# Where ScalarE saves a scan's last column, when the FFN runs, and who multiplies behind a gelu

## The chip, the cores and the metric

The kernel runs on one core of a Trainium2 chip. The metric is the device time of one execution in microseconds (us), as the median of several runs. The core has five queues that work side by side and meet only at semaphores: TensorE (PE), VectorE (DVE), ScalarE (ACT), GpSimd (POOL), and SyncE (SP), which here issues nearly all DMAs. Each queue runs its own instructions strictly in program order.

## The reference

Eight images of 64 channels and 128x128 pixels go through two layers. The first is a filter whose nine taps per pixel come from a small convolution and a softmax. The second is a bidirectional Mamba block between convolutions, followed by a gated feed-forward part (FFN). What matters here is the scan of the Mamba block and the FFN:

```python
def selective_scan(u, dt, A, Bm, Cm, D, z):
    dt = jax.nn.softplus(dt)
    dA = jnp.exp(jnp.einsum('bdl,dn->bldn', dt, A))
    dBu = jnp.einsum('bdl,bnl,bdl->bldn', dt, Bm, u)
    ...
    _, hs = jax.lax.associative_scan(comb, (dA, dBu), axis=1)
    y = jnp.einsum('bldn,bnl->bdl', hs, Cm) + D[None, :, None] * u
    return y * jax.nn.silu(z)
...
xn = ln4d(x, norm2_w, norm2_b)
g = conv2d(xn, ffn_in_w, pad=0)
g = conv2d(g, ffn_dw_w, groups=2 * HID, pad=1)
g1, g2 = jnp.split(g, 2, axis=1)
g = jax.nn.gelu(g1, approximate=False) * g2
return x + conv2d(g, ffn_out_w, pad=0)
```

There are 128 inner channels `d` and 16 states `n` for each of 16384 pixels, two directions and two layers per image: for every channel and state a recurrence `h = dA * h + dBu` runs along the pixels, and its values are multiplied by `C` and summed over the states.

## The kernel before

**Chunks and steps.** The scans are the backbone. A chunk is 1024 pixels (`T`) of one image, layer and direction; there are 16 chunks per scan, 64 per image, 512 in all. A chunk's 128 channels times 16 states are 2048 rows, done as 16 steps of 128 rows (`U` = 16), so an image has 1024 steps (`IMAGE`). Step `u` of a chunk does the following:

- `decay` (L1226), two steps ahead: ScalarE writes `w = exp(dt * A)` into one of two PSUM tiles, in turn;
- `drive` (L1218): GpSimd computes `bu` for two steps in one instruction, some steps ahead, into four buffers;
- `scan` (L1245 forward, L1247 backward): VectorE runs the recurrence over `w` and `bu`, starting from the state column that the chunk before it left;
- `product`: the scan's values times `C`. Where `on_pool(u)` is true, the scan has written to SBUF (`hs`) and GpSimd multiplies one step later (L1264, L1266). Elsewhere the scan has written over `w` in PSUM, which GpSimd is not given, and VectorE multiplies (L1262);
- `keep` (L1269): ScalarE copies the last column of the scan, one value per row, to the state for the next chunk, 16 steps on;
- `collect` (L1284): PE sums two steps' products over the states.

`on_pool` (L1207) is true for steps 0, 2 and 6 of every eight, except right behind a step in which a gelu is planned (`gelu_times`): there VectorE keeps step 6's product. So a chunk has six products on GpSimd and ten on VectorE, in some chunks one more on VectorE.

**The order.** Nothing is left to a scheduler. `at(time, phase, fn)` puts every piece of work at a step and a phase, and at the end they are emitted in the order of step and phase: FEED, SCAN, MID, PROD, EXP, DECAY, REST. Within a step and phase the order is that of planning: the chunks first, in their order, then the rest. The position in this list decides the order in each engine's queue; waits between engines are put in by the tile layer where two instructions use the same tile. For a step whose product is on VectorE, product and copy both stand in phase PROD, product first; then come the decay for two steps on (EXP), outputs of other work on ScalarE (DECAY) and everything else (REST).

**Around the scan.** Each chunk is prepared during the 32 steps ahead of it: convolution, silu (L1119, and L1121 for the gate in the second of the two directions; planned at step 11 of a 16, REST) and softplus (L1148, step 2 of a 16, REST). Silu, softplus and gelu each need another ScalarE table than exp, so each loads a table before and the exp table again after (L68). Loads of `dup`, `dtp`, `bp` and `cp` for the next chunk go out on SP's queue at fixed steps.

**Beside the scan** run, on the same queues, the work of other images: `Front` (the first layer and norms of the next image, from step 593 - 24 of an image on, one piece every 24 steps), `Mix` (from 990 on, every 13 steps) and `Ffn` (`FFN_AT` = 1202, that is step 178 of the next image, every 24 steps, 16 pieces). Of the last image nothing is left to run beside, so its `Ffn` runs `alone`, after the scans, with other steps.

**One Ffn piece**, planned from step `a`: four window DMAs at a-4 and a-3 (`load`); the convolution of the first channel group at a to a+3, copied out at a+5 (`first_out`, L962); of the rest at a+6 to a+9; gelu at a+11 (`gelus`, L969 and L971, with the table loads); the rest's product at a+13 (`rest_times`, L976); the second group's convolution at a+14 to a+17; its two products at a+19 and a+21 (`times`, L979); two loads at a+16 (`load_x2`); the projection at a+21 (`project`, L994 to L1000), copied out and stored at a+23 (`add`, `store`).

Of the kernel before, what the change touches and what calls it, by code (L numbers as in the profile page):

```python
# [21 lines left out]
NCH = HALF // ROWS  # L22
# [14 lines left out]
FEED, SCAN, MID, PROD, EXP, DECAY, REST = range(7)  # L37

IMAGE = 4 * NT * U
FRONT_STEP, MIX_STEP, FFN_STEP = 24, 13, 24  # L40
FRONT_AT, MIX_AT, FFN_AT = 593, 990, 1202

SILU, SOFTPLUS, GELU = 11, 18, 11

# [11 lines left out]
def kernel(ctx: ExitStack, tc: tile.TileContext, a: dict, out: bass.AP):  # L56
# [6 lines left out]
    nc = tc.nc  # L63
    x = a["x"]
    B = x.shape[0]
# [122 lines left out]
    with tc.tile_pool(name="wspill", bufs=1) as fp, tc.tile_pool(name="wprep", bufs=2) as pp, \  # L188
            tc.tile_pool(name="wps", bufs=4, space=PSUM) as pps:
        with tc.manual_schedule():  # L190
# [161 lines left out]
            for l in range(DEPTH):  # L352
# [9 lines left out]
                for d in range(2):  # L362
                    cw, xdt, xbc, dtn, al, dp = dirs[2 * l + d]
                    taps = by_taps(inx2, cw, DI, KC)
                    for j in range(KC):
                        t = turned(taps[:, j, :], ident, P, DI)
                        at = j if d == 0 else KC - 1 - j
# [39 lines left out]
    def at(time, phase, fn, *args):  # L407
        steps.setdefault((time, phase), []).append((fn, args))
# [466 lines left out]
    class Ffn:  # L875
# [139 lines left out]
        def plan(self, a):  # L1015
            early = 12 if self.alone else 0
            at(a - 4 - early, REST, self.load, 0)
            at(a - 3 - early, REST, self.load, 1)

            if self.alone:  # L1020
                at(a - 6, REST, self.before_taps)
                at(a - 5, DECAY, self.before_taps_out)
                at(a - 5, REST, self.taps, 0)
                at(a - 2, REST, self.taps, 1)
                groups = ((0, 0, self.first_out, 2), (3, 1, self.times, 6))
                gelus, out = 3, 9
            else:
                groups = ((0, 0, self.first_out, 5), (6, 2, None, 0), (14, 1, self.times, 19))
                gelus, out = GELU, 21
            for t, g, end, to in groups:  # L1030
                for i in range(4):
                    at(a + t + (0 if self.alone else i), REST, self.conv, g, i)
                for h in range(2 if end else 0):
                    late = 0 if self.alone or end == self.first_out else 2 * h
                    at(a + to + late, MID if end == self.times else DECAY, end, h)
            at(a + gelus, REST, self.gelus)
            at(a + gelus + 2, MID, self.rest_times)
            at(a + out - 5, REST, self.load_x2)
            at(a + out, REST, self.project)
            at(a + out + 2, DECAY, self.add)  # L1040
            at(a + out + 2, REST, self.store)
# [7 lines left out]
            Ffn(b, c).plan(a + step * c)  # L1049


    gelu_times = {IMAGE * b + FFN_AT + FFN_STEP * c + GELU for b in range(B - 1) for c in range(NCH)}
    up, down = list(range(NT)), list(reversed(range(NT)))
    order = []
    for b in range(B):
# [4 lines left out]
    class Chunk:  # L1060
# [143 lines left out]
        def on_pool(self, u):  # L1204


            if u % 2 or u % 8 == 4 or self.t0 + u - 1 in gelu_times:  # L1207
                return False
            return True

# [55 lines left out]
                nc.gpsimd.tensor_tensor(out[:, ::-1], hs[:, ::-1], c[:, ::-1], ALU.mult)  # L1266

        def keep(self, u):
            nc.scalar.copy(self.column(u), self.last(self.hs.pop(u)))  # L1269

        def collect(self, k):

# [72 lines left out]
        def plan(self):  # L1345
            b = self.t0 - 2 * U

            def feed(t, fn, *args):
                if self.beside_front:
                    at(t, FEED, fn, *args)  # L1350
                else:
                    at(t - 1, REST, fn, *args)

            at(b + (5 if self.i == NCH - 2 else 3), REST, self.load_hn)
            for h in range(2):
                feed(b + 7 + h, self.conv, h)
                at(b + 7 + h, DECAY, self.conv_out, h)
                if self.second:
                    feed(b + 9 + h, self.gate, h)
                    at(b + 9 + h, DECAY, self.gate_out, h)  # L1360
                feed(b + 14 + h, self.step, h)
                at(b + 14 + h, DECAY, self.step_out, h)
            at(b + SILU, REST, self.silu)
            at(b + SOFTPLUS, REST, self.softplus)
            if self.second:
                at(b + 13, REST, self.store_gate)
            b = self.t0
            feed(b - 16, self.bc)
            at(b - 16, DECAY, self.bc_out)
            at(b - 14, REST, self.store_bc)  # L1370
            at(b - 13, REST, self.store_dt)
            at(b - 11, FEED, self.dtx)
            at(b - 10, REST, self.store_du)
            j0 = self.pairs[0][0] // 2
            at(b - 10, REST, self.load_states, "bp", j0)
            at(b - 8, REST, self.load_channels, "dup", 0)
            at(b - 6, REST, self.load_channels, "dtp", 0)
            at(b - 5, REST, self.load_states, "bp", 1 - j0)
            at(b - 4, REST, self.load_states, "cp", j0)
            at(b - 3, REST, self.load_channels, "dup", 1)  # L1380
            at(b - 2, REST, self.load_channels, "dtp", 1)
            at(b - 1, REST, self.load_states, "cp", 1 - j0)
            for k in range(U // 2):
                at(b + 2 * k - 5, REST, self.drive, k)
                at(b + 2 * k + 3 + (k % 4 == 0), REST, self.collect, k)
            for u in range(U):
                at(b + u - 2, EXP, self.decay, u)
                at(b + u, SCAN, self.scan, u)
                at(b + u + self.on_pool(u), FEED if self.on_pool(u) else PROD, self.product, u)
            for u in range(U):  # L1390
                at(b + u + self.on_pool(u), EXP if self.on_pool(u) else PROD, self.keep, u)
            for h in range(2):
                if self.second:
                    at(b + 8 * h + 1, REST, self.load_yf, h)
                    at(b + 8 * h + 6, REST, self.add_yf)
                    at(b + 8 * h + 7, REST, self.load_gate, h)
                if self.second:
                    at(b + 8 * h + 11, MID, self.y_out, h)
                else:
                    at(b + 8 * h + 10, DECAY, self.y_out, h)  # L1400
                    at(b + 8 * h + 11, REST, self.store_y, h)
            if not self.second:
                return
            b += U
            n = self.norm
            at(b + 2, REST, self.load_h)
            feed(b + 5, self.project)
            at(b + 6, DECAY, self.residual)
            at(b + 6, DECAY, self.square)
            if self.l == 0:  # L1410
                at(b + 7, REST, self.store_h)
            feed(b + 12, lambda: n.means(mm_tile, self.sq))
            at(b + 13, DECAY, n.means_out)
            feed(b + 17, n.spread, mm_tile)
            at(b + 19, MID, self.normed)
            if self.l:
                at(b + 20, DECAY, self.weighted)
            at(b + 20, REST, self.store_hn)
# [10 lines left out]
    for b in range(B):  # L1429
        a, last = IMAGE * b, b == B - 1  # L1430
# [36 lines left out]
```

## Time and profile before

| | us |
|---|---|
| median of 3 runs | 28348.76 (28341.41 to 28352.17) |
| the profiled execution | 28355.4 |
| its span, first to last instruction | 28353.5 |
| first scan starts | 386.1 |
| last scan starts | 27928.9 |
| one image's 1024 steps, images 2 to 7 | 3450.9 to 3457.7 |
| mean of one scan, L1245 and L1247 | 2.34 |
| VectorE's product, L1262 | 1.222 |
| GpSimd's product, L1264 and L1266 | 2.37 |
| GpSimd's drive, L1218 | 4.548 |
| ScalarE's decay, L1226 | 1.119 |
| ScalarE's copy of the last column, from `w` and from `hs` | 0.158 and 0.178 |
| a table load | 1.283 |

The rows of the profile give start, duration, engine, line, operation, and output and input tiles; in brackets stands how long the engine was idle before, and what ended that. `state<-w` is the copy behind a scan whose product VectorE makes, `state<-hs` one whose product GpSimd makes. The granted TensorE clock was 0.883 on average.

### The profile page before, as it was taken

The numbers are of one execution on the slowest core, as the hardware profiler recorded it, in microseconds if no ns is written. First come the engines' busy times: TensorE is split into PE (matmuls) and PEld (weight loads), VectorE is DVE, ScalarE is ACT, GpSimd is POOL, SyncE is SP. The second block draws the span as 40 slices with busy tenths as digits, with TensorE's granted clock in tenths as the row PEclk, the third lists the DMA queues.
The fourth block names the chain that finished last, engine by engine and source line by source line (L and its number), as shares of the span: only waits on it lengthen the run. The fifth ranks groups of instructions, "written<-read, shape, count | busy, mean of one in ns | idle before, by whom it ended". The sixth has DMA issues, their size and how long they took to land. (4 is left out here: it accounts for less than half of the span.)

```text
span 28353.5 us, 311709 instructions
## 1 busy us (share of the span) xinstructions
PE 23008.2 (81%) x98188; PEld 7334.6 (26%) x98188; DVE 26988.0 (95%) x17438; ACT 18798.4 (66%) x29139; POOL 26586.1 (94%) x7980
## 2 busy tenths in 40 slices
PE   7666888878888788887888888887888878888679
PEld 3212322223222232222322223222222222222113
DVE  6999999999999999999999999999999999999997
ACT  4666666666666666666666666666666666666663
POOL 4999999999999999999999999999999999999994
PEclk7777889988899888988889888998888988899789
DMA  6777787777877678777787777777777777777675
GB/s 161 232 242 228 236 261 249 248 228 240 264 245 250 226 237 270 242 248 229 244 261 247 240 231 248 258 248 240 234 250 251 250 237 234 255 254 251 216 250 155
DMA packets 2611073, 6796.34 MB, mean 240 GB/s; under 512 B 433558, under 2 KB 739110, under 8 KB 2608390
## 3 DMA queue, kind: packets, MB, share of 16 engines
q1 hardware_dynamic: 2608534, 6776.25, 73.7%
q8 instruction: 776, 12.71, 0.2%
q14 instruction: 883, 7.23, 0.1%
q10 hardware_dynamic: 880, 0.14, 0.0%
HBM read 5543.05 MB, written 1265.19 MB: 240 GB/s over the span
## 5 line engine op out<-in xcount | busy, mean ns | idle before, releaser
L1218 POOL TENSOR_TENSOR bu<-dup,bp 128x2048 f32<-128x2048 f32 x4096 | 18594.4, 4548 | 52.2 <-DMA dup<-du_dram 26.1
L1226 ACT ACTIVATE w<-dtp,a_neg 128x1024 f32<-128x1024 f32 x8192 | 9163.6, 1119 | 1429.0 <-DVE hs L1247 601.6
L1262 DVE TENSOR_TENSOR hs<-w,cp 128x1024 f32<-128x1024 f32 x5232 | 6391.1, 1222 | 199.0 <-DMA cp<-bc_dram 46.6
L1247 DVE TENSOR_TENSOR_SCAN w<-w,state,bu 128x1024 f32<-128x1024 f32 x2651 | 6210.2, 2343 | 88.6 <-ACT w L1226 58.7
L1245 DVE TENSOR_TENSOR_SCAN w<-w,state,bu 128x1024 f32<-128x1024 f32 x2581 | 6048.2, 2343 | 121.8 <-ACT w L1226 105.0
L1284 PE MATMUL y<-hs,sel_y 128*32 128x512 f32 x32768 | 4944.7, 681 | 569.3 <-POOL hs L1266 445.5
L1269 ACT COPY state<-w 128x1 f32<-128x1 f32 x5232 | 828.0, 158 | 5178.4 <-DVE hs L1262 5119.6
L1264 POOL TENSOR_TENSOR hs<-hs,cp 128x1024 f32<-128x1024 f32 x1515 | 3593.5, 2372 | 428.4 <-DVE hs L1245 286.3
L1266 POOL TENSOR_TENSOR hs<-hs,cp 128x1024 f32<-128x1024 f32 x1445 | 3424.5, 2370 | 395.1 <-DVE hs L1247 351.8
L1245 DVE TENSOR_TENSOR_SCAN hs<-w,state,bu 128x1024 f32<-128x1024 f32 x1515 | 3550.6, 2344 | 151.9 <-ACT state L1269 79.3
L1247 DVE TENSOR_TENSOR_SCAN hs<-w,state,bu 128x1024 f32<-128x1024 f32 x1445 | 3384.5, 2342 | 78.0 <-ACT state L1269 43.0
L1093 PE MATMUL xp<-hn,wx 128*128 128x512 f32 x4096 | 2494.0, 740 | 1188.3 <-ACT xc L1099 567.8
L914 PE MATMUL fp<-fw,bgw 128*128 128x512 f32 (+1 forms) x5760 | 2118.5, 613 | 38.1 <-DMA fw<-xn_dram 34.0
L1135 PE MATMUL dp<-xc,wdt 128*128 128x512 f32 x2048 | 1331.6, 737 | 710.3 <-ACT dt L1142 392.1
L1284 PEld LDWEIGHTS y<-hs,sel_y 128*32 128x32 f32 x32768 | 720.2, 114 | 4256.0 <-issue 2609.4
L1277 PE MATMUL y<-xc,dskip 128*64 128x512 f32 x4096 | 1358.9, 748 | 415.9 <-ACT yv L1301 323.5
L1093 PEld LDWEIGHTS xp<-hn,wx 128*128 128x128 f32 x4096 | 845.8, 225 | 2679.6 <-issue 1047.3
L68 ACT ACT_TABLE_LOAD x1137 | 1458.8, 1283 | 20.8 <-PEq L1456 0.7
L1099 ACT ACTIVATE xc<-xp,cbias 128x512 f32<-128x512 f32 x1024 | 701.2, 685 | 1159.3 <-PE xp L1093 1156.5
L920 PE MATMUL fp<-fw,bgw 64*128 64x512 f32 (+1 forms) x5760 | 1379.1, 605 | 0.0
L607 PE MATMUL wb<-wt,sel_k 65*128 65x512 bf16 x1152 | 508.8, 442 | 1000.7 <-DVE t L611 994.3
L622 PE MATMUL acc<-t,ident 128*128 128x512 f32 x2160 | 1307.2, 693 | 0.0
(220 smaller groups left out, 26231.9 us busy)
## 6 DMA issues: line engine op xcount, KB each, us to landing
bp<-bc_dram SPq DMA_DIRECT2D x4096, 256.0 KB, 4.2
dup<-du_dram SPq DMA_DIRECT2D x4096, 256.0 KB, 5.2
dtp<-dt_dram SPq DMA_DIRECT2D x4096, 256.0 KB, 5.1
cp<-bc_dram SPq DMA_DIRECT2D x4096, 256.0 KB, 4.9
hn<-hn_dram SPq DMA_DIRECT2D x1024, 256.5 KB, 4.4
dt_dram<-dt SPq DMA_DIRECT2D x512, 512.0 KB, 3.0
du_dram<-du SPq DMA_DIRECT2D x512, 512.0 KB, 2.6
yf_dram<-yv SPq DMA_DIRECT2D x512, 256.0 KB, 3.1
```

The costliest lines, as they stand in the source:

```text
L68: nc.scalar.preload_act_table_set("natural_log_exp_and_others")
L914: nc.tensor.matmul(o, wpair[:, i, g, m], self.win[h][:, i : i + ROWS, 0:W], start=(i == 0), stop=False)
L920: nc.tensor.matmul(o, wlast[rows, i, g, m], self.win[h][rows, i : i + ROWS, lo : W + lo], start=False, stop=(i == 2),)
L1093: nc.tensor.matmul(self.xp[h], wx[:, self.l, self.d, i, :], self.hn2[:, s.start + 2 * i : s.stop + 2 * i], start=(i == 0), stop=(i == 1),)
L1218: nc.gpsimd.tensor_tensor(bu, self.dup[self.pairs[k][1]], self.over_pair("bp", k), ALU.mult)
L1226: nc.scalar.activation(w, self.dtp[gp][:, i, :], AF.Exp, scale=a_neg[:, self.l, self.d, g, j : j + 1])
L1245: nc.vector.tensor_tensor_scan(to, w, bu, s0, ALU.mult, ALU.add)
L1247: nc.vector.tensor_tensor_scan(to[:, ::-1], w[:, ::-1], bu[:, ::-1], s0, ALU.mult, ALU.add)
L1262: nc.vector.tensor_tensor(out, hs, c, ALU.mult)
L1264: nc.gpsimd.tensor_tensor(out, hs, c, ALU.mult)
L1266: nc.gpsimd.tensor_tensor(out[:, ::-1], hs[:, ::-1], c[:, ::-1], ALU.mult)
L1284: nc.tensor.matmul(self.y[lo : lo + 32, :], sel_y, hs[:, i, s], start=False, stop=(k % 4 == 3))
```

## The change

Three things are edited.

1. `keep` of a step whose product is on VectorE moves from phase PROD to phase MID, so that it is emitted in front of the product; it no longer takes the scan's output out of the table `self.hs`, since the product reads it after. The copy of a step whose product is on GpSimd stays where it was.
2. `FFN_AT` goes from 1202 to 1204, so each `Ffn` piece beside the scans runs two steps later: its gelu at step 7 of every eight in place of 5. Inside a piece, both products (`times`) come at a+20, the rest's product at a+14, the projection at a+20 with its loads at a+15, and its copy and store at a+22. The last image's pieces stay as they were.
3. `gelu_times` is gone: GpSimd makes the products of steps 0, 2 and 6 of every eight without exception.

```diff
-FRONT_AT, MIX_AT, FFN_AT = 593, 990, 1202
+FRONT_AT, MIX_AT, FFN_AT = 593, 990, 1204
...
-                groups = ((0, 0, self.first_out, 5), (6, 2, None, 0), (14, 1, self.times, 19))
-                gelus, out = GELU, 21
+                groups = ((0, 0, self.first_out, 5), (6, 2, None, 0), (14, 1, self.times, 20))
+                gelus, out = GELU, 20
             for t, g, end, to in groups:
                 for i in range(4):
                     at(a + t + (0 if self.alone else i), REST, self.conv, g, i)
                 for h in range(2 if end else 0):
-                    late = 0 if self.alone or end == self.first_out else 2 * h
-                    at(a + to + late, MID if end == self.times else DECAY, end, h)
+                    at(a + to, MID if end == self.times else DECAY, end, h)
             at(a + gelus, REST, self.gelus)
-            at(a + gelus + 2, MID, self.rest_times)
+            at(a + gelus + (2 if self.alone else 3), MID, self.rest_times)
...
-    gelu_times = {IMAGE * b + FFN_AT + FFN_STEP * c + GELU for b in range(B - 1) for c in range(NCH)}
...
-            if u % 2 or u % 8 == 4 or self.t0 + u - 1 in gelu_times:
+            if u % 2 or u % 8 == 4:
                 return False
             return True
...
         def keep(self, u):
-            nc.scalar.copy(self.column(u), self.last(self.hs.pop(u)))
+            nc.scalar.copy(self.column(u), self.last(self.hs[u]))
...
             for u in range(U):
-                at(b + u + self.on_pool(u), EXP if self.on_pool(u) else PROD, self.keep, u)
+                at(b + u + self.on_pool(u), EXP if self.on_pool(u) else MID, self.keep, u)
```

In the changed file the lines behind the removed `gelu_times` stand two earlier: decay L1224, product L1260, GpSimd's product L1262 and L1264, copy L1267.

## The prediction

> **What bounds the kernel now.** I read the totals first, then one whole image's stretch, then who waits for whom on VectorE and ScalarE, then the rows of single steps.
>
> ```profile
> PE 23008.2 (81%) x98188; PEld 7334.6 (26%) x98188; DVE 26988.0 (95%) x17438; ACT 18798.4 (66%) x29139; POOL 26586.1 (94%) x7980
> ```
>
> ```profile
> 7303.00:10757.00 3454.00, 2862.18 (x12336) 911.82 (x12336) 3332.68 (x2116) 2347.36 (x3632) 3315.28 (x993) 0.90 0.75 245
> ```
>
> The second fence is the stretch of one image in the middle (after the length: PE, PEld, DVE, ACT, POOL busy). VectorE works 3332.68 of 3454 us and GpSimd 3315.28, so a microsecond added to VectorE's queue is a microsecond on the time, whatever the stage: VectorE is idle only 121 us per image. GpSimd is nearly as full. ScalarE has a third of its time free, but its queue is strictly in order, and this change turns on when it is free.
>
> ```profile
> ACT state L1269 <- DVE hs L1262: 5119.6, 3159, 8.4
> ...
> DVE w L1245 <- ACT w L1226: 105.0, 111, 2.7
> ...
> DVE hs L1245 <- ACT state L1269: 79.3, 100, 1.2
> DVE hs L1245 <- ACT w L1226: 68.9, 53, 3.4
> DVE w L1247 <- ACT w L1226: 58.7, 76, 1.8
> ```
>
> These are waits: total us, times, longest. The first row is the pair that the change turns round. A scan that GpSimd does not multiply writes over its decays `w` in PSUM; VectorE's product (L1262) and ScalarE's copy of the last column (L1269) both only read that `w`, and still the copy waits for the product, 3159 of 5232 times. So the two reads of one PSUM tile are kept apart, in program order. The other 2073 copies did not wait: there ScalarE came later than the product's end, over 1.2 us after the scan. Today nobody needs the copy for 16 steps, and the decay behind it is needed two steps on, so VectorE hardly notices (the four last rows).
>
> **Copy in front of the product (phase MID).** Phases are emitted in order, so now the copy comes first and the product waits for it. In the order in which the changed kernel's instructions stand, each of the 5120 products left on VectorE waits for ScalarE, and no other order changes on ScalarE by this edit, since MID holds no other ScalarE work. Behind the waiting product in VectorE's queue stands the next scan; GpSimd's products, PE's sums over `hs` and SP's reloads of `cp` wait for these in turn, so they move along with it. The price is in ScalarE's queue at the moment the scan ends. Softplus:
>
> ```profile
> 13996.99 1.12 ACT L1226 ACTIVATE w<-dtp,a_neg 128x1024 f32<-128x1024 f32 x1
> 13998.13 1.28 ACT L1148 ACT_TABLE_LOAD   x1
> 13999.42 1.06 ACT L1148 ACTIVATE dt<-dt 128x1024 f32<-128x1024 f32 x1
> 14000.50 1.28 ACT L68 ACT_TABLE_LOAD   x1
> 14001.79 0.16 ACT L1269 COPY state<-w 128x1 f32<-128x1 f32 x1
> ...
> 13996.38 2.33 DVE L1245 TENSOR_TENSOR_SCAN w<-w,state,bu 128x1024 f32<-128x1024 f32 x1
> 13998.62 0.67 DVE L1330 TENSOR_TENSOR hn<-h,rb 128x512 f32<-128x512 f32 x1
> 13999.21 0.68 DVE L1299 TENSOR_TENSOR yv<-y,gate 128x512 f32<-128x512 f32 x1
> 13999.80 1.22 DVE L1262 TENSOR_TENSOR hs<-w,cp 128x1024 f32<-128x1024 f32 x1
> ```
>
> The product started at 13999.80; its copy could run only at 14001.79. With the copy first, the product starts at 14001.79 + 0.16 + 0.03 = 14001.98: 2.2 us late. Silu:
>
> ```profile
> 5155.53 1.28 ACT L1119 ACT_TABLE_LOAD   x1
> 5156.82 1.06 ACT L1119 ACTIVATE xc<-xc 128x1024 f32<-128x1024 f32 x1
> 5157.78 1.04 ACT L1121 ACTIVATE gate<-gate 128x1024 f32<-128x1024 f32 x1
> 5158.84 1.28 ACT L68 ACT_TABLE_LOAD   x1
> 5160.14 0.16 ACT L1269 COPY state<-w 128x1 f32<-128x1 f32 x1
> ...
> 5153.98 2.35 DVE L1247 TENSOR_TENSOR_SCAN w<-w,state,bu 128x1024 f32<-128x1024 f32 x1
> 5156.37 1.23 DVE L1262 TENSOR_TENSOR hs<-w,cp 128x1024 f32<-128x1024 f32 x1
> ```
>
> Here 5156.37 becomes 5160.33: 4.0 us. There are 512 chunks, each with one of either.
>
> Sum over the run, ten VectorE products per chunk of 16 steps:
>
> 1. *Silu*, step 12: from the release of ScalarE (end of product 11) decay 1.12, copy 0.17, two table loads and silu 3.62, the gate's silu 1.04 in half of the chunks (0.52), against the scan's 2.27: 3.16, plus the turn-round below, 3.4 with odd small operations. 512 × 3.4 = 1740 us.
> 2. *Softplus*, step 3: 1.12 + 3.62 + half a `yv` copy of 0.58 − 2.25 = 2.8, plus 0.2, less the VectorE work that in second passes already stands between scan and product (0.58 + 0.59, so 0.6 on average and partly behind other waits): 2.2, as in the window. 512 × 2.2 = 1130 us.
> 3. *Turn-round* at the eight others: scan end to product start is 0.03 us now (VectorE after itself); then it is 0.03 to ScalarE (product end to copy start above 14004.54 to 14004.57), 0.16 copy, 0.03 back: 0.19 more. Where VectorE has other work between scan and product (by its rows 1667 of 5232) it costs nothing. 8 × 0.68 × 0.19 × 512 = 530 us; if that cover is gone, 780.
> 4. *Short ScalarE operations held up by PE*, in front of the copy: ScalarE's waits for PE at `xc` (1156.5 us), `dt` (204.4), `gate` (155.7), `bc` (122.0). Adding up the rows between each decay and the next copy against the scan's length: 160 us over all eight places if these waits shrink to nothing, 850 if they stay, 2680 if every copy stays as late against its scan as it is now. I take 850, the same queue as now without the lateness that is carried on from step to step, because a product that waits for ScalarE brings the two level again.
> 5. *Gelu*: next part, 260.
>
> Together 4510 us. What it gives back: the waits of scans for copies (79.3 + 43.0 + 15.3 + 15.2) and decays (105.0 + 68.9 + 58.7 + 8.0), 393 us, go, since the product has waited already.
>
> The Trainium skill, "PSUM — Partial Sum Buffer", section "PSUM bank collisions raise a hardware error", speaks against the change: two engines reading one bank and partition at once collide like a write would, and the compiler's scheduler therefore orders ScalarE's and VectorE's accesses. The row of 3159 waits shows it one way round only, the copy behind the product; by the rule the product behind the copy waits too, and without it the sum would be that of the faster rival below. The page "ScalarE: Activation LUTs", section "What ACT_TABLE_LOAD costs", gives a load 1283 ns and then about 1380 ns of drain. The rows show 1.28 and the next operation 0.01 us behind it; by the page the two lumps would be up to 4 × 1.38 × 512 = 2830 us dearer (an estimate). The sum goes by the rows.
>
> **GpSimd keeps the product behind a gelu.** 112 products (7 images × 16) leave VectorE: from start to next start 1.14 us (14003.31 to 14004.45), −128 us. On GpSimd they are 112 × 2.37 = 265 us, hidden by its idle time, which grows with every VectorE stall above (now 135 us per image); without that cover they are +265.
>
> **FFN two steps later; products both at step 20, rest product a step later, projection a step earlier.** The gelu (two loads 2.56, 0.60, 1.14: 4.3 us) moves to step 7 or 15 of a chunk, so a GpSimd product follows; the next VectorE product is two scans off. ScalarE has 1.12 + 4.3 + 1.12 + some 0.8 = 7.3 against 2 × 2.27 = 4.5, so 2.6 late, less the cover of what is there already: 2.3 × 112 = 260 us; bounds 0 (all in term 4) and 3.4 × 112 = 380. `times` sees `fp` a step later or earlier: at most the 47.6 us of its present waits. The moved DMAs, 4 window loads, 2 loads and 2 stores per FFN chunk and one of weights per image, pass `cp`, `bp` and `dup` loads on SP's queue; a window lands in 5.1 us and is needed four steps on, some 13 us, so nothing, or the 34.0 us of waits for `fw` again. First-out and the convolutions move with them: PE, 81% busy, nothing.
>
> **Sum.** 4510 − 128 − 393 = +3990 us on the profiled 28355: 32345, or, that execution being 7 us above the median, **32340 us**.
>
> **Bounds.** Low: term 4 at 160, gelu at 0, and VectorE's present waits for PE (158.6 + 99.4 + 51.3 + 47.6 + 25.2 + 19.9 = 402) covered too: +2640, 30990. High: term 4 at 2680, the lumps as late as in the rows (+290), gelu 380, nothing given back: +6620, 34980.
>
> **Rivals.**
> - *Only the turn-round* (0.07): ScalarE catches up before each scan ends. 530 − 128, less up to 393: 28360 to 28760. Against it: 4 table loads per chunk stand right in front of VectorE products.
> - *Carried lateness* (0.08): the high bound, 34,000 to 35,000; for it, the 2073 copies that are late today; against it, each stall lets ScalarE catch up.
> - *Faster* (0.04): copies run under VectorE's other work and the product never waits, ScalarE's 5119.6 us of waiting goes, and with it 393 + 128 = 521 us: 27830. It decides if the mean added wait per product is under 521 / 5120 = 0.10 us; the copy alone is 0.16, so it needs the reads to go together after all.
> - *GpSimd becomes the bound* (0.01): +265 with no VectorE stall, 28620; against it, VectorE stalls first.
>
> **How the numbers follow.** Forecast 0.80, between 30,600 and 34,000; the range is that, with the first rival, the third, and most of the second left out. A measurement of this kernel tells some 0.2% (57 us) from no change: faster 0.04, same 0.02 (the cheap end of the first rival), slower 0.94.
>
> **What would show it.** In the new profile: ScalarE's wait for VectorE's product at L1267 gone, replaced by one for the scan; VectorE's product (L1260) idle before it some 3 to 5 ms, released by the copy, the longest 4 to 5 us and most of it behind table loads; VectorE near 83%, GpSimd near 83%, their busy sums almost unchanged; GpSimd products 3072 in place of 2960. Waits of products below 1 ms in total would prove the forecast wrong, and so would a chunk (16 steps, now 54 us) that is not some 7 to 8 us longer in all stages alike.

## The result and the profile after

The changed kernel takes 32693.62 us (median, 32689.78 to 32696.46) against 28350.25 us for the kernel before beside it: 1.153 times as long, 95% interval 1.1519 to 1.1547. The forecast was 32340. Of the runs further down one, of the kernel with the copy first at steps 3 and 12 alone, took 32731 us at a granted clock of 0.683 (the others of that kernel 0.853 to 0.856) and is left out. The page's totals of the changed kernel:

```profile
span 32693.2 us, 307213 instructions
...
PE 24256.5 (74%) x98188; PEld 7710.5 (24%) x98188; DVE 26844.8 (82%) x17326; ACT 18817.1 (58%) x29139; POOL 26882.7 (82%) x8092
```

The work is the same: VectorE's busy sum fell by 143 us (112 products less), GpSimd's rose by 297, ScalarE's by 19. TensorE's rose by 1248 with the same 98188 matmuls, at a mean granted clock of 0.842 in place of 0.883. So the 4340 us that the span grew by are not work of VectorE or GpSimd; both were nearly full and fell to 82%. The waits (engine, line, what it waited for; total us, times, longest) say where:

```profile
ACT w L1224 <- DVE hs L1260: 6779.0, 5088, 2.7
DVE hs L1260 <- ACT state L1267: 5367.1, 4244, 7.7
...
ACT state L1267 <- DVE w L1245: 1379.4, 1436, 1.8
```

The pair is turned round. The copy no longer waits for the product (it waits for the scan, third row and its forward twin), and 4244 of VectorE's 5120 products wait for the copy, 5367 us in all. What ScalarE used to wait at the copy it now waits one instruction later, at the decay (first row), which needs the same `w` free: nothing was won there. A chunk took 53.8 us on average and takes 62.3. The growth is not the same in all stages: averaged over eight chunks it lies between 6 and 10 us, and the first image, beside which no FFN runs, takes 452 us longer, each of the others 550 to 569. VectorE's other waits shrink: for TensorE at L642 from 99.4 to 28.7 us, and its idle time before scans from 440 us (395 of it for ScalarE) to 8.

One silu in the timeline of the changed kernel, ScalarE's rows and then VectorE's (start, duration, and in brackets the idle time before and what ended it):

```profile
9844.55 1.28 ACT L1117 ACT_TABLE_LOAD   x1
9845.84 1.06 ACT L1117 ACTIVATE xc<-xc 128x1024 f32<-128x1024 f32 x1
9846.81 1.04 ACT L1119 ACTIVATE gate<-gate 128x1024 f32<-128x1024 f32 x1
9847.87 1.28 ACT L68 ACT_TABLE_LOAD   x1
9849.16 0.16 ACT L1267 COPY state<-w 128x1 f32<-128x1 f32 x1
9850.61 1.12 ACT L1224 ACTIVATE w<-dtp,a_neg 128x1024 f32<-128x1024 f32 x1 [1.29 <-DVE hs L1260]
...
9843.19 2.35 DVE L1245 TENSOR_TENSOR_SCAN w<-w,state,bu 128x1024 f32<-128x1024 f32 x1
9849.35 1.23 DVE L1260 TENSOR_TENSOR hs<-w,cp 128x1024 f32<-128x1024 f32 x1 [3.82 <-ACT state L1267]
```

The scan is done at 9845.54. Its last column, 0.16 us of copying, stands behind 4.6 us of table loads and silu, and VectorE stands with it: copy end 9849.32, product 9849.35.

By step of the chunk, VectorE's waits in front of its products, summed over the trace (us):

| kernel | 1 | 3 | 4 | 9 | 12 | 13 | 5, 7, 11, 15 | 6, 14 |
|---|---|---|---|---|---|---|---|---|
| before | 12 | 0 | 54 | 0 | 19 | 0 | 0 | 4 |
| changed | 703 | 1204 | 96 | 1040 | 1744 | 86 | 494 | none there |

### The profile page after: what moved, and what is told of

Read it like the earlier page. It is cut to its first block, busy times and chain, and to the rows that moved or that the text cites. A ratio compares the mean times of both kernels' runs of the same rounds, so it can differ in the third digit from the quotient of the medians.

```text
span 32693.2 us, 307213 instructions
## 1 busy us (share of the span) xinstructions
PE 24256.5 (74%) x98188; PEld 7710.5 (24%) x98188; DVE 26844.8 (82%) x17326; ACT 18817.1 (58%) x29139; POOL 26882.7 (82%) x8092
## 5 line engine op out<-in xcount | busy, mean ns | idle before, releaser
L1224 ACT ACTIVATE w<-dtp,a_neg 128x1024 f32<-128x1024 f32 x8192 | 9161.0, 1118 | 8649.1 <-DVE hs L1260 6779.0
L1260 DVE TENSOR_TENSOR hs<-w,cp 128x1024 f32<-128x1024 f32 x5120 | 6263.1, 1223 | 5367.2 <-ACT state L1267 5367.1
L1243 DVE TENSOR_TENSOR_SCAN w<-w,state,bu 128x1024 f32<-128x1024 f32 x2560 | 5997.0, 2343 | 0.6 <-ACT w L1224 0.6
L1245 DVE TENSOR_TENSOR_SCAN w<-w,state,bu 128x1024 f32<-128x1024 f32 x2560 | 5995.7, 2342 | 0.0
L1264 POOL TENSOR_TENSOR hs<-hs,cp 128x1024 f32<-128x1024 f32 x1536 | 3623.6, 2359 | 2335.5 <-DVE hs L1245 1844.2
L1262 POOL TENSOR_TENSOR hs<-hs,cp 128x1024 f32<-128x1024 f32 x1536 | 3615.0, 2354 | 2187.1 <-DVE hs L1243 1555.3
L1282 PE MATMUL y<-hs,sel_y 128*32 128x512 f32 x32768 | 5254.2, 695 | 130.1 <-DVE hs L1260 129.7
L1243 DVE TENSOR_TENSOR_SCAN hs<-w,state,bu 128x1024 f32<-128x1024 f32 x1536 | 3598.7, 2343 | 5.2 <-ACT w L1224 3.4
L1245 DVE TENSOR_TENSOR_SCAN hs<-w,state,bu 128x1024 f32<-128x1024 f32 x1536 | 3596.5, 2341 | 2.1
L1133 PE MATMUL dp<-xc,wdt 128*128 128x512 f32 x2048 | 1497.2, 821 | 2123.6 <-ACT r L495 1022.8
L914 PE MATMUL fp<-fw,bgw 128*128 128x512 f32 (+1 forms) x5760 | 2391.6, 658 | 203.8 <-DVE gt L976 172.9
L1267 ACT COPY state<-w 128x1 f32<-128x1 f32 x5120 | 810.7, 158 | 2589.1 <-DVE w L1245 1379.4
L502 PE MATMUL rb<-ident,r 128*64 128x128 f32 x12288 | 1031.2, 320 | 802.1 <-ACT r L496 275.1
L920 PE MATMUL fp<-fw,bgw 64*128 64x512 f32 (+1 forms) x5760 | 1484.2, 635 | 0.0
L1097 ACT ACTIVATE xc<-xp,cbias 128x512 f32<-128x512 f32 x1024 | 700.5, 684 | 1163.9 <-PE xp L1091 1163.9
```

Source lines behind the costliest of these rows:

```text
L914: nc.tensor.matmul(o, wpair[:, i, g, m], self.win[h][:, i : i + ROWS, 0:W], start=(i == 0), stop=False)
L920: nc.tensor.matmul(o, wlast[rows, i, g, m], self.win[h][rows, i : i + ROWS, lo : W + lo], start=False, stop=(i == 2),)
L1133: nc.tensor.matmul(self.dp[h], wdt[:, self.l, self.d, :], self.xc[:, halves[h]], start=True, stop=True)
L1224: nc.scalar.activation(w, self.dtp[gp][:, i, :], AF.Exp, scale=a_neg[:, self.l, self.d, g, j : j + 1])
L1243: nc.vector.tensor_tensor_scan(to, w, bu, s0, ALU.mult, ALU.add)
L1245: nc.vector.tensor_tensor_scan(to[:, ::-1], w[:, ::-1], bu[:, ::-1], s0, ALU.mult, ALU.add)
```

## The experiments

Every time is given with its ratio to the kernel before, run beside it, and the ratio's interval.

**Taking the copy back.** Only the copy's phase is undone; the FFN and GpSimd stay as changed.

```diff
-                at(b + u + self.on_pool(u), EXP if self.on_pool(u) else MID, self.keep, u)
+                at(b + u + self.on_pool(u), EXP if self.on_pool(u) else PROD, self.keep, u)
```

> The changed kernel with the copy back in phase PROD, behind the product; the FFN times and GpSimd's product behind a gelu stay as changed. Theory (the order of copy and product is all of the cost): the time falls back to 28,150 to 28,450 us, with no wait of VectorE's product for the copy; the 112 products that left VectorE are worth up to 128 us, GpSimd's 265 us more take some of that away. Rival (the later FFN, or GpSimd's 112 products, carry a part of the loss): over 28,600 us, with the difference in the image steps 178 to 566 alone.

28596.35 us, 1.008 (1.0065 to 1.0095). So 4097 of the 4343 us are the order of copy and product. But the theory's band ended at 28,450, and the time is just under the rival's 28,600: the rest of the change is no gain, it loses 0.8% by itself. The loss is beside the FFN, as the rival had it: the first image takes 3462.4 us in both kernels. In the timeline of this kernel, a gelu at step 15, ScalarE first:

```profile
15252.14 1.28 ACT L969 ACT_TABLE_LOAD   x1
...
15255.09 1.28 ACT L68 ACT_TABLE_LOAD   x1
15256.38 1.12 ACT L1224 ACTIVATE w<-dtp,a_neg 128x1024 f32<-128x1024 f32 x1
...
15250.16 2.33 DVE L1245 TENSOR_TENSOR_SCAN w<-w,state,bu 128x1024 f32<-128x1024 f32 x1
15252.53 1.23 DVE L1260 TENSOR_TENSOR hs<-w,cp 128x1024 f32<-128x1024 f32 x1
15257.59 2.35 DVE L1245 TENSOR_TENSOR_SCAN hs<-w,state,bu 128x1024 f32<-128x1024 f32 x1 [3.84 <-ACT w L1224]
```

The decay behind the gelu ends at 15257.50, and the scan that needs it, the third one behind the gelu's step, starts then. Over the run this scan waits 353 us in 112 places; before it waited nowhere. Which part of the change does that is taken up below.

**The copy alone.** The kernel before, with the copy in phase MID and not taken out of its table, nothing else:

```diff
-                at(b + u + self.on_pool(u), EXP if self.on_pool(u) else PROD, self.keep, u)
+                at(b + u + self.on_pool(u), EXP if self.on_pool(u) else MID, self.keep, u)
```

> The kernel before with the copy in phase MID, in front of VectorE's product, and nothing else. Theory: the whole loss and a little more, 32,500 to 33,100 us, since 112 products stay on VectorE (+128 us) and stand right behind a gelu (3.4 us of waiting each, 380 us, against some 345 us that the gelus cost at their new place). Rival (the later FFN carries a part): below 32,200 us.

32567.28 us, 1.1479 (1.1462 to 1.1497): in the band, at its low end. Its waits:

```profile
DVE hs L1262 <- ACT state L1269: 5135.2, 4020, 5.8
```

Steps 6 and 14 wait 390 us here, 3.5 us behind each gelu, as expected; steps 1 and 9 wait 1189 in place of 1743.

**The copy at steps 3 and 12 alone, and at all others alone.** `else MID if u in (3, 12) else PROD`, and the reverse.

> The kernel before with the copy in front of the product only at steps 3 and 12 of a chunk, those behind softplus and silu. In the changed kernel these two places waited 1204 and 1744 us. Theory (a wait is there what ScalarE's table loads leave over, place by place): 28350 + 2950, less some 200 us that scans no longer wait for decays, so 30,900 to 31,300 us, with waits of about 2.3 us at step 3 and 3.4 us at step 12. Rival (the turn-round between the engines is the cost, alike at every product): a fifth of the loss, about 29,200 us.

> The kernel before with the copy in front of the product at all steps of a chunk but 3 and 12. Theory with catching up (a product that waits brings ScalarE level, so that lateness not taken at step 12 or 3 is met again at 13 and 4): more than the 2420 us that these places waited in the changed kernel, by some 500 to 1,000 us at steps 13 and 4; less some 200 us given back, so 30,900 to 31,600 us, and the losses of this kernel and of the one with steps 3 and 12 alone together exceed that of all steps by 500 us or more. Rival (places add up): 30,200 to 30,700 us, the two losses adding up to the whole.

Steps 3 and 12 alone: 31098.21 us, 1.0961 (1.0943 to 1.0979), in the band. The others alone: 30284.36 us, 1.0675 (1.0657 to 1.0693), below the theory's band and in the rival's. The waits, first kernel and second:

```profile
DVE hs L1262 <- ACT state L1269: 3133.2, 1005, 5.7
```

```profile
DVE hs L1262 <- ACT state L1269: 2745.9, 3139, 6.1
```

| kernel | 1 | 3 | 4 | 9 | 12 | 13 | 5, 7, 11, 15 | 6, 14 |
|---|---|---|---|---|---|---|---|---|
| copy first everywhere | 297 | 1207 | 96 | 892 | 1744 | 73 | 435 | 390 |
| at 3 and 12 | 0 | 1252 | 15 | 0 | 1881 | 0 | 0 | 4 |
| at all others | 280 | 0 | 359 | 771 | 19 | 503 | 453 | 390 |

Two steps, a fifth of the products, cost 2726 us by themselves, with some 1000 waits of 3.1 us on average; leaving them out of the whole saves 2283 of its 4195. So the cost is not a turn-round that is alike at every product. The catching up is there: where step 12 does not wait, step 13 pays 503 instead of 73, and step 4 pays 359 instead of 96. The two losses together are 4639 us, 443 more than the whole: so the losses do not simply add up, as the rival had it, but the surplus is a little under the theory's 500. What my band for the second kernel missed was not this but what is given back: of its 2746 us of waits only 1912 reach the time, since other waits of VectorE go away when the chunk gets longer. I had allowed 200 us.

**VectorE makes the copies.**

```diff
-            nc.scalar.copy(self.column(u), self.last(self.hs[u]))
+            copy = nc.scalar.copy if self.on_pool(u) else nc.vector.tensor_copy
+            copy(self.column(u), self.last(self.hs[u]))
```

> The changed kernel, its copies in front of VectorE's products made by VectorE itself; the copies of GpSimd's steps stay on ScalarE. Theory (the loss is that VectorE now waits for another engine's queue): the waits of products for copies go, 5120 copies of one column on VectorE come. Nearest rows: memset of 128x16 0.07 us, the smallest copies out of PSUM 0.18 us, so 0.1 to 0.25 us each with the wait of the product for it, 510 to 1280 us on the 28,596 us of the kernel with the product first: 28,900 to 29,900 us. Rival (a copy of the same PSUM tile in front of the product costs, whoever makes it): over 32,000 us.

28825.76 us, 1.016 (1.0146 to 1.0174), even a little under the band. The groups of VectorE (count, busy us, mean ns, idle before):

```profile
L1260 DVE TENSOR_TENSOR hs<-w,cp 128x1024 f32<-128x1024 f32 x5120 | 6235.4, 1218 | 70.3 <-DMA cp<-bc_dram 41.3 <-issue 3.8 <-DMA bc_dram<-bc 3.6
...
L1268 DVE COPY state<-w 128x1 f32<-128x1 f32 x5120 | 805.9, 157 | 167.2
```

The same copy of the same column in front of the same product, in VectorE's own queue: VectorE idles 70 us before its products in place of 5367. It is the other engine's queue that costs, not the copy. Against the kernel with the product first it costs 229 us, 0.045 us for each copy of 0.157.

**Without the convolution of the second half.** `conv(1)` returns the first half's PSUM tile and issues no matmuls.

> The changed kernel without TensorE's convolution of a chunk's second half: ScalarE takes the first half's sums twice, so the second half of xc is left out of the computation, ScalarE's work is the same and it no longer waits for PE in step 8. Theory (the 1040 us of waits at step 9 are ScalarE waiting for that convolution, which itself waits for ScalarE to empty the only PSUM tile): the waits at step 9 fall to some 200 to 350 us, those behind a gelu staying, and the time to 31,750 to 32,100 us. Rival (ScalarE is late there by its own work): within 200 us of 32,694.

32200.19 us, 1.1347 (1.1331 to 1.1362): the time fell by 493 us, a little less than the theory's 600 to 940. ScalarE's waits at `xc` fell from 1163.9 to

```profile
ACT xc L1100 <- PE xp L1094: 320.3, 194, 5.2
```

and those of products at step 9 from 1040 to 444, while step 11 rose from 116 to 251. So somewhat over half of step 9 is ScalarE waiting for that convolution. The 444 that are left are more than the theory's 200 to 350: 189 us of them are behind gelus, and the remaining 250 were not taken apart.

**Without the table loads of silu and softplus.** Both become exp, and the loads of the exp table behind them go.

> The changed kernel with exp in place of silu and of softplus, so that neither loads a table (the functions themselves are left out; gelu stays). ScalarE's lumps shrink by 2.57 us each and everything else stays. Theory (a wait is what ScalarE's work in front of the copy leaves over the scan): step 12 from 3.41 to about 0.85 us, 440 us; step 3 from 2.35 to 0.2 to 0.5 us, 100 to 250 us; with that 30,300 to 30,800 us. Rival (the lumps only take the place of other lateness that then shows): over 31,500 us.

30024.1 us, 1.0581 (1.0565 to 1.0597). Step 12 waits 344 us in place of 1744, step 3 137 in place of 1204. In all:

```profile
DVE hs L1258 <- ACT state L1265: 2643.2, 3889, 6.2
```

The two places lost 2467 us of waiting, all products together 2724, and the time fell by 2670, beyond the band's 2390. The wait at step 12 went from 3.41 to 0.67 us, by 2.74; the two rows of 1.28 that left make 2.57.

**GpSimd's product alone.** The kernel before without `gelu_times`:

```diff
-            if u % 2 or u % 8 == 4 or self.t0 + u - 1 in gelu_times:
+            if u % 2 or u % 8 == 4:
```

> The kernel before with GpSimd making also the product behind a gelu, the FFN and the copies as before. The kernel with everything changed but the copies took 28,596 us, 224 more than before beside it; scans waited 415 us longer, at steps 2 and 10. Theory (that loss is ScalarE's lateness behind a gelu, which the VectorE product at the next step used to cover): scans two and three steps behind a gelu wait some 2 us more each, the 112 products give 128 us back, 28,350 to 28,600 us. Rival (GpSimd, nearly full, carries its 265 us): GpSimd idle under 1% beside the FFN and VectorE's scans waiting for bu, 28,500 to 28,640 us, the waits naming bu.

28358.01 us, 0.9994 (0.9985 to 1.0003): no difference. GpSimd's products are 3072 as in the changed kernel:

```profile
L1266 POOL TENSOR_TENSOR hs<-hs,cp 128x1024 f32<-128x1024 f32 x1536 | 3637.7, 2368 | 166.1 <-DVE hs L1247 124.3 <-DMA xa<-x_dram 14.8 <-DMA dup<-du_dram 10.1
L1264 POOL TENSOR_TENSOR hs<-hs,cp 128x1024 f32<-128x1024 f32 x1536 | 3633.9, 2366 | 380.8 <-DVE hs L1245 247.3 <-PE op L1313 48.5 <-issue 40.1
```

VectorE's work is 125 us less, but it idles 112 us more, 73 of them before the third scan behind a gelu. None of these waits ended with ScalarE, which the theory had expected: 34 us ended with GpSimd's rows, 38 with nothing that the profile shows. GpSimd's products took 254 us more (7271.6 against 7018.0); the kernel is no longer for it, and no shorter for what VectorE saves.

**The rest of the loss without the copy: gelu's place, GpSimd, or the order inside a piece.** Two kernels on the one with the product first: one gives the 112 products behind a gelu back to VectorE (`gelu_times` again, at the gelu's new place); the other puts `FFN_AT` back to 1202.

> The changed kernel with the copies behind the products again, as in the one of 28,596 us, and with VectorE making again the 112 products behind a gelu (steps 0 and 8 of a chunk at the gelu's new place). In that kernel the third scan behind each gelu waits 3.15 us for its decay, 353 us in all. Theory (the loss is ScalarE's lateness behind a gelu in steps 7 and 15): the extra product covers 1.14 us of each such wait and costs as much, the wait falls to some 2.0 us and the time stays, 28,500 to 28,660 us. Rival (GpSimd's 112 products are the loss): back to 28,320 to 28,420 us.

> The kernel of 28,596 us (copies behind the products, all else as changed) with the FFN two steps earlier again, so the gelu is at step 5 or 13; both products at step 20 of a piece, the rest's product and the projection stay as changed, GpSimd keeps the product behind a gelu. Theory (the gelu's new step is the loss): no scan waits 3 us three steps behind a gelu, 28,300 to 28,450 us. Rival (the order inside a piece, which holds the PSUM tile of the rest a step longer, is the loss): over 28,550 us.

The first: 28579.04 us, 1.0078 (1.0065 to 1.009). The third scans behind a gelu wait 225 us in place of 353, 2.0 each, and the time stays, as the theory had it. The second: 28383.46 us, 1.0009 (1.0 to 1.0018), with 122 us of those waits. So the 0.8% is the FFN's new place, two steps later: not GpSimd's products, and not the order inside a piece. The third scans' waits, 353 against 122 us, differ by about as much as the times do; the gelu was not moved apart from the rest of its piece.

## Why the prediction came out right, and where its terms were off

The mechanism is the one forecast, and it is shown from both sides: undoing the copy's place takes 4097 us away, making only that change brings 4195. That the product waits for the copy as the copy waited for the product, which the trace of before could not show, has its row: 4244 waits. By terms:

1. *Silu*, 1740 us forecast, 1744 waited, and 1744 again in the kernel with the copy alone.
2. *Softplus*, 1130 forecast, 1204 waited, 2.35 us each. The items of that sum give 2.4; the 2.2 that went into it was taken from the one window.
3. *Turn-round*, 530 forecast. Where ScalarE was free in time the median wait of a product is 0.23 us (steps 5, 7, 13, 15), the 0.19 of the forecast with the 0.03 that was there before. The term has no sum of its own in the trace: steps 4, 5, 7, 11, 13 and 15 waited 676 us together, turn-round and short lateness.
4. *Short operations held up by PE*, 850, and 5. *gelu*, 260: here the sum was too low. With the turn-round they were 1640; these eight steps waited 2419. Step 9 is most of it. I had counted PE's waits as they stood and let the carried lateness go. At steps 4 and 13 it did go: before, ScalarE is free for the copy 0.73 and 1.33 us after the scan's end on average, and now in time. At step 9 it did not: 1.79 us before in chunks with no gelu near, and a wait of 1.59 now in the 400 chunks where nothing of the FFN stands in front. The reason can be read in one such step of the changed kernel, ScalarE, VectorE and TensorE:

```profile
10641.25 0.68 ACT L1097 ACTIVATE xc<-xp,cbias 128x512 f32<-128x512 f32 x1
...
10645.44 0.69 ACT L1097 ACTIVATE xc<-xp,cbias 128x512 f32<-128x512 f32 x1 [1.95 <-PE xp L1091]
10646.02 0.15 ACT L1267 COPY state<-w 128x1 f32<-128x1 f32 x1
...
10642.25 2.33 DVE L1245 TENSOR_TENSOR_SCAN w<-w,state,bu 128x1024 f32<-128x1024 f32 x1
10646.21 1.22 DVE L1260 TENSOR_TENSOR hs<-w,cp 128x1024 f32<-128x1024 f32 x1 [1.62 <-ACT state L1267]
...
10641.98 3.42 PE L1091 MATMUL xp<-hn,wx 128*128 128x512 f32 x4 [6.75 <-ACT xc L1097]
```

ScalarE empties the first half's PSUM tile (the kernel has one for both), PE may only then compute the second half into it, and ScalarE waits for that with the copy behind it. That lateness is a chain through PE and does not shrink when ScalarE is brought level, so "catching up" did not apply there. The kernel without the second half shows this for somewhat over half of it. Behind the gelus the waits were 3.41 us (step 9) and 5.47 (step 1), 497 in all; the same steps of the 13th to 36th chunk of the first image, where no FFN runs beside, would give 111. So the gelu cost 386; I had 260, and there my own items give 2.8 us late where I wrote 2.6.
6. *Given back*: 393 forecast. The scans' idle time fell from 440 to 8 us, as forecast. But by the sum, 5367 less the 89 that products waited before, less 128, less the span's 4340, some 810 us came back. The missing part is mainly VectorE's other waits, which I had put into the low bound alone (402): for PE 575 before and 372 now, for DMAs (products apart) 45 and 2. The rest is mostly gaps of 0.03 us between a scan and its product, which the waits now contain.

The waits were 857 us above the 4510 of the sum; 89 of them were there before, and 417 more than forecast came back. That leaves the difference of some 350 us. Each of the two errors is larger than the difference; that the total came within 1.1% is in part luck. Of the signs that the prediction named, three were missed: products waited 5.4 ms and not 3 to 5, the longest 7.7 us and not 4 to 5, and a chunk grew by 6 to 10 us, most beside the FFN, and not by 7 to 8 in all stages alike.

*The two small parts.* "First-out and the convolutions move with them: PE, 81% busy, nothing" was wrong. With the copy first the two parts cost 127 us together, 32694 against 32567 for the copy alone: VectorE's busy sum is 100 us lower, and products wait 232 us more. The gelu is not the reason, since it costs the same at either place: 390 us at steps 6 and 14 in the kernel with the copy alone, 386 here. New are the products 18 steps behind a gelu, which is five steps into the next piece. They wait 374 us in 112 places (steps 1 and 9), where the same steps of the first image would give 111. In the kernel with the copy alone the products 18 steps behind a gelu stand at steps 7 and 15 and wait 25 us, no more than in the first image. One of the 112, at step 9, TensorE and ScalarE:

```profile
13962.56 1.93 PE L914 MATMUL fp<-fw,bgw 128*128 128x512 f32 x4
...
13966.47 1.98 PE L1091 MATMUL xp<-hn,wx 128*128 128x512 f32 x4
...
13968.50 0.69 ACT L1097 ACTIVATE xc<-xp,cbias 128x512 f32<-128x512 f32 x1 [4.00 <-PE xp L1091]
```

ScalarE had emptied the tile at 13963.49, but in TensorE's queue the FFN's convolution (L914 and L920) and a sum over states stood in front of the second half, and the product waited 4.29 us. This is read from the traces; no run moves that convolution alone.

With the copy where it was, the FFN's new place loses some 210 us (28596 against 28383), because the decay behind the gelu, not the copy, is then what VectorE waits for; the forecast had no case for that. "GpSimd's 265 us are hidden" is right, even without the stalls that I had named as their cover, but in the kernel that shows it the 128 us that VectorE saves do not show either.

*The rivals.* "Only the turn-round" fell with the two lumps' 2726 us; "carried lateness" was right for step 9 and wrong for 4 and 13 (96 and 86 us); "faster" needed waits under 0.10 us per product, and they were 1.05; "GpSimd becomes the bound" fell with the kernel in which GpSimd's 112 products come alone and change nothing.

## What to carry to other kernels

An instruction that another engine must wait for inherits the whole queue in front of it: before a small copy is moved ahead on one engine, look at what stands before it there at that moment (here two table loads), not at its own 0.16 us. Where two engines read the same PSUM tile, the order in which they are written down decides who waits; let the fuller engine go first, or do both on it. And when a block of work is moved, each of its parts meets new neighbours in its engine's queue: here the gelu a decay that was needed, and the convolution a matmul that ScalarE waited for. Which instruction behind each part is needed first is the question to ask before.

## What the runs showed of the hardware that was not expected

VectorE's copy of one column out of PSUM has a row of 157 ns, but 5120 of them cost 229 us of time, 45 ns each. VectorE's busy time grew by 524 us, 0.10 for each copy, since neighbouring rows overlap, and its idle time fell by 263, most of it before scans (855 to 576); whether that is because ScalarE has fewer copies was not tried.

The granted TensorE clock was lower in the kernels that wait more, though TensorE did the same work: 0.883 before, 0.879 with the product first, 0.856 with waits at steps 3 and 12, 0.842 in the changed kernel. But it was lowest, 0.822, in the kernel that leaves a convolution out, whose products wait less than the changed kernel's (4887 against 5367 us); so less work for TensorE did not raise it, and the waits alone do not set it. From the kernel before to the changed one the matmuls of `dp` went from 737 to 821 ns on average. Whether that lengthened step 9's chain by more than the 0.1 us by which the mean second half grew (2.30 to 2.40 us) was not tried.
